# The last unit's exponentials and loads in another order, and the top-1 low-rank rows on four quarters of the partitions

## The chip, the cores and the metric

The kernel runs on one core of a Trainium2 chip. The core has five engines with queues of their own: TensorE (PE, and PEld for its weight loads), VectorE (DVE), ScalarE (ACT), GpSimd (POOL) and SyncE (SP), which here only issues DMAs. Each engine works through its own queue in order. The metric is device time in microseconds of one execution. The kernel before took 1837.35 us (median of three runs, 1833.86 to 1838.45).

## The reference

Two blocks in a row work on 1024 tokens of 512 features in fp32. The first is a linear-memory attention and a top-2 mixture of low-rank experts over a common dense matrix. The second, which matters here, is a state-space layer and a top-1 mixture:

```python
x = x + _L1_attn_ref(_layernorm(x), ...)   # state-space layer: 128 heads of 64, chunks of 128 tokens
x = x + _L1_ffn_ref(_layernorm(x), ...)    # 4 experts of rank 8, the best one per token
```

In the state-space layer the input is projected to a gate, to x, B and C (each with a causal convolution of 4 taps and a silu) and to time steps. With `A_cumsum`, the running sums of the time steps times A, it computes for each head

```python
Lmat = jnp.exp(segment_sum(Ac))                    # decays between positions of a chunk
M = Gm * jnp.transpose(Lmat, (0, 2, 3, 4, 1))      # times the products of C and B
Y_diag = jnp.einsum('bclsh,bcshp->bclhp', M, xch)
```

and adds what the chunk before hands on, scales by an RMS norm over all 8192 channels, multiplies by silu(gate) and projects back to 512 features. The mixture at the end is

```python
top1 = jnp.argmax(logits, axis=-1)
base_out = jnp.einsum('bth,oh->bto', x, W_up)
z = jnp.einsum('nh,erh->ner', x_flat, lora_A)      # 4 x 8 = 32 low-rank rows for each token
d = jnp.einsum('ner,ehr->neh', z, lora_B) * SCALE
delta = jnp.einsum('neh,ne->nh', d, one_hot)       # only the chosen expert's
```

## The kernel before

**Units.** The state-space layer runs as 72 units: eight groups, each with one "bc" unit (B and C) and eight "pair" units (two heads each). Units are staggered. While the loop of line 948 projects unit n (`stage_a`, seven products on sums of operands, L529), it multiplies unit n-2 (`stage_c`, L751 and L759) and finishes it (`stage_d`, L777 and L778), transposes unit n-1 (`stage_t`, L695, with L698 and L705 on VectorE) and computes its decays. The last unit is n = 71; units 69, 70 and 71 are all pair units.

**Decays.** For each pair unit a tile `cst` (128 x 2 x 12 x 128) is filled from HBM with the running sums by one broadcast DMA of 1536 KB (`load_sums`, L646, two buffers). `decays(n, part)` turns it into the decay matrix: parts 0 and 1 are eight Relus each with a bias (L728), part 2 is two exponentials on ScalarE (L734) and two products with the group's matrix on VectorE (L736). `stage_c` reads the result. In the steady state part 2 is traced at the end of unit n+1, behind the silus of `stage_a`.

**Output products.** The projection back is done over the units as well, as seven products per pair of output matrices (L836) in PSUM. `add_up` copies each to SBUF on ScalarE (L845, three buffers called `prod`) and POOL issues a DMA that accumulates it in HBM (L846, `prod_d`, 256 KB each). PSUM holds two of these products at a time (tag `mm1`). The last unit has the last seven products, of half m = 0: three are copied in its first half and four in its second. At the end `load_prods` reads the products back (L860, L861, four DMAs for each half m, on SP), and `put_together` adds them: m = 1 on POOL, m = 0 on VectorE (L868 to L874). The last four pairs do not go through these products; they are multiplied plainly after the units (`out_project`, L1040).

**The order of the work.** A planner lays out each engine's queue: it goes by the order in which the program traces the instructions and takes a later one first where an earlier one is not ready by its own costs. `issue_after(ins)` keeps what is traced inside it behind `ins` on the engine of `ins`; that is how the order is written out by hand. `last` holds the instructions that serve for this. `behind_keeps` holds silus of the convolution (L580) until `let_go` issues them behind the `keep` copies.

**After the units** come, in program order: the Relus of unit 71, its silu, the eight reads, stages C and D of unit 70, two pairs of `out_project` for four tiles of tokens, the transposes of unit 71, the third pair, `put_together(1)`, stages C and D of unit 71, `put_together(0)`, the rest of `out_project`, the sums for the RMS norm (L1068), and then per tile of 128 tokens the last pair, the read-back parts (L1082), the residual and a layer norm (`finish`).

**The mixture** is `lora_mixture` (L148). For each of eight tiles of tokens it computes logits and low-rank rows in one product (L160), copied to `lg` and `h`. `h` is 128 wide per tile, and for the last layer (32 rows) the rest is set to zero. `base` (L174) multiplies a tile with the dense matrix, four products of 128 x 512; three tiles are taken ahead. `route` finds the best expert, L187 zeroes the other experts' rows, eight transposes (L190) and one copy (L191) turn `h`, and one product per tile (L193) adds the low-rank part in the same PSUM bank as its base. L196 adds the residual and `store` writes the tile. `f1_up`, the 32 rows of `lora_B`, sits on the first 32 of 128 partitions, the rest zero (L1027). PSUM has eight banks: four under the tag `in`, two under `mm1` and one pair under `mm2`.

Of the kernel before, what the change touches and what calls it, by code (L numbers as in the profile page):

```python
# [28 lines left out]
F32 = mybir.dt.float32  # L29
AF = mybir.ActivationFunctionType  # L30
ALU = mybir.AluOpType
AX = mybir.AxisListType

P = 128
# [19 lines left out]
def model_kernel(ctx: ExitStack, tc: tile.TileContext, a: dict, out: bass.AP):  # L54
# [93 lines left out]
    def lora_mixture(name, E, R, w_base, w_cat, w_up, route, psum, pool, done, ready=None):  # L148

        ER = E * R  # L150
        lg = pool.tile([P, NT, E], F32, tag="lg", name=f"{name}_lg")
        h = pool.tile([P, NT, P], F32, tag="e", name=f"{name}_h")
        if ER < P:
            nc.gpsimd.memset(h, 0.0)
        for t in range(NT):
            if ready:
                ready(t)
            ps = psum.tile([P, 512], F32, tag="mm1", name=f"{name}_psl{t}")
            for k in range(KT):
                nc.tensor.matmul(  # L160
                    ps[:, : E + ER],
                    lhsT=xnT[:, k, toks(t)],
                    rhs=w_cat[:, k, :],
                    start=(k == 0),
                    stop=(k == KT - 1),
                )
            nc.vector.tensor_copy(lg[:, t, :], ps[:, :E])
            nc.vector.tensor_copy(h[:, t, :ER], ps[:, E : E + ER])
        hT = pool.tile([P, NTOK], F32, tag="sig", name=f"{name}_hT")
# [15 lines left out]
        cmb = route(lg)  # L185
        hv = h[:, :, :ER].rearrange("p t (e r) -> p t e r", r=R)
        nc.vector.tensor_tensor(hv, hv, cmb.unsqueeze(3).to_broadcast([P, NT, E, R]), ALU.mult)  # L187
# [4 lines left out]
        for t in range(NT):  # L192
            nc.tensor.matmul(held[t], lhsT=hT[:, toks(t)], rhs=w_up, start=False, stop=True)  # L193
            if t + ahead < NT:
                held[t + ahead] = base(t + ahead)
            nc.vector.tensor_tensor(x[t], held.pop(t), x[t], ALU.add)  # L196
            done(t)


# [155 lines left out]
    with ExitStack() as c1:  # L355
# [11 lines left out]

        last = {"pe": None, "one": None, "two": None, "adt": None, "bar": None, "keep": None, "cst": None, "silu": None}

# [270 lines left out]
        def load_sums(n):  # L640

            kind, j = units[n]
            if kind == "bc":
                return
            cst = b2.tile([P, 2, NT + NB, P], F32, tag="cst", name=f"cst{j}")
            nc.sync.dma_start(  # L646
                out=cst.rearrange("p h c l -> p h (c l)"),
                in_=cs_d[2 * j : 2 * j + 2, :].unsqueeze(0).to_broadcast([P, 2, (NT + NB) * P]),
            )
            held[n].update(cst=cst)  # L650
# [66 lines left out]
        def decays(n, part):  # L717
# [15 lines left out]
            for hh in range(2):  # L733
                nc.scalar.activation(mf[:, hh], mf[:, hh], AF.Exp, scale=-1.0)  # L734
            for hh in range(2):
# [212 lines left out]
        for n in range(len(units)):  # L948
# [22 lines left out]
            with issue_after(last["keep"]):  # L971
                add_up()
                if steady:
                    decays(n - 1, 1)
            turn(n, 1)
            next(a_steps)
            out_products(share - share // 2)
            add_up()
            if share and not todo:
# [14 lines left out]
        N = len(units)  # L994
        for part in range(2):
            decays(N - 1, part)
        let_go()
        load_prods(1)
        load_prods(0)
        with issue_after(last["pe"]):  # L1000
# [15 lines left out]
        class PsumF:  # L1016
            @staticmethod
            def tile(shape, dt, tag, name):
                if "ln_ps" in name or "psl" in name:
                    return two_banks[0][:, int("psl" in name)]  # L1020
                return Psum.tile(shape, dt, {"mm2": "mm2", "mm1": "in"}[tag], name)

# [3 lines left out]
        f1_up = b3.tile([P, DM], F32, tag="sg", name="f1_up")  # L1026
        nc.gpsimd.memset(f1_up, 0.0)  # L1027
        nc.sync.dma_start(out=f1_up[:32, :], in_=a["f1_up"])
        x_v = x_d.rearrange("(t p) d -> p t d", p=P)
# [129 lines left out]
```

## Time and profile before

| What | Value |
|---|---|
| Median of three runs | 1837.35 us (1833.86 to 1838.45) |
| Profiled execution | 1835.83 us, of which the span is 1834.0 us |
| Mean granted TensorE clock | 0.993 |
| TensorE busy | 1787.6 us, 97% of the span |
| VectorE, ScalarE, POOL busy | 1295.6, 1195.4, 713.2 us |
| TensorE's longest single wait | 9.1 us, `ps_y` L751 for `cst` L736, until 1736.6 |
| From the last logits product (about 1800.7) to the end | 33 us |

Times inside the span are in microseconds from its start. A row of the order of time gives start, duration, engine, line, instruction, tile written and tiles read, and in brackets the engine's idle time before it with what ended it. Where instructions of a kind follow each other, they are merged and counted (x8). An fp32 matmul shows as two records, and records of matmuls overlap, so that their durations add up to more than the time they take together. A row of windows gives a stretch, its length, for each engine the busy time and the number of instructions, the clock granted to TensorE as a share of full speed, the busy share of the DMA engines and the rate that they moved.

### The profile page before, as it was taken

The numbers are of one execution on the slowest core, as the hardware profiler recorded it, in microseconds if no ns is written. First come the engines' busy times: TensorE is split into PE (matmuls) and PEld (weight loads), VectorE is DVE, ScalarE is ACT, GpSimd is POOL, SyncE is SP. The second block draws the span as 40 slices with busy tenths as digits, with TensorE's granted clock in tenths as the row PEclk, the third lists the DMA queues.
The fourth block names the chain that finished last, engine by engine and source line by source line (L and its number), as shares of the span: only waits on it lengthen the run. The fifth ranks groups of instructions, "written<-read, shape, count | busy, mean of one in ns | idle before, by whom it ended". The sixth has DMA issues, their size and how long they took to land.

```text
span 1834.0 us, 21364 instructions
## 1 busy us (share of the span) xinstructions
PE 1787.6 (97%) x7670; PEld 940.2 (51%) x7670; DVE 1295.6 (71%) x1470; ACT 1195.4 (65%) x2145; POOL 713.2 (39%) x691
## 2 busy tenths in 40 slices
PE   7999988999999999999999999999999999999799
PEld 4545544555555555555555555545555555555464
DVE  4524798876777777767877687867786877587462
ACT  4311259776878588847875787678766876687730
POOL 5410242344444444443345434534453444443310
PEclk9999999999999999999999999999999999999899
DMA  8100133454466555555565556554655565556811
GB/s 318 65 1 10 49 127 125 154 156 111 121 163 151 134 138 144 144 144 143 147 152 144 109 152 156 145 133 116 149 147 141 147 146 144 110 147 169 213 48 46
DMA packets 81338, 241.05 MB, mean 131 GB/s; under 512 B 9584, under 2 KB 10608, under 8 KB 71888
## 3 DMA queue, kind: packets, MB, share of 16 engines
q1 hardware_dynamic: 48768, 171.49, 27.0%
q0 software_dynamic: 31888, 67.14, 22.2%
q8 instruction: 61, 1.00, 0.2%
q10 hardware_dynamic: 576, 1.05, 0.2%
q14 instruction: 45, 0.37, 0.1%
HBM read 177.78 MB, written 61.87 MB: 131 GB/s over the span
## 4 chain that ended last, share of the span: by engine, by line
PE 88%; DVE 5%; ACT 3%; DMA 2%; issue 1%; POOL 1%; SPq 0%; DVEq 0%; POOLq 0%; ACTq 0%
PE pa L529 25%; PE ps_p L836 19%; PE pd L529 12%; PE pb L529 6%; PE ps_y L751 5%; PE f_pso L174 3%; PE ps_q L97 3%; PE ps_o L309 3%; PE ps_xt L695 3%; PE ps_y L759 2%; DVE xT L572 1%; ACT cst L728 1%; DMA cst<-cs_d 1%; PE f_pso L193 1%; DMA prod_d<-prod 1%
## 5 line engine op out<-in xcount | busy, mean ns | idle before, releaser
L846 POOL DMA_DIRECT2D prod_d<-prod x217 | 190.3, 915 | 575.7 <-ACT prod L845 554.4
L728 ACT ACTIVATE cst<-cst,cs 128x128 f32<-128x128 f32 x1024 | 313.0, 398 | 4.5 <-DMA cst<-cs_d 4.5
L572 DVE SCALAR_TENSOR_TENSOR xT<-raw,convw,xT 128x1020 f32<-128x1020 f32 (+2 forms) x216 | 278.1, 1289 | 4.1
L736 DVE TENSOR_TENSOR cst<-cst,gt 128x1536 f32<-128x1536 f32 x128 | 221.2, 1756 | 19.3 <-ACT cst L734 19.1
L514 POOL TENSOR_TENSOR wsum<-win 128x256 f32<-128x256 f32 x72 | 112.3, 1560 | 265.8 <-DMA win<-in_win 223.6
L769 ACT ACTIVATE xdt<-xT 128x1024 f32<-128x1024 f32 x64 | 67.7, 1058 | 197.7 <-DVE xT L767 197.7
L734 ACT ACTIVATE cst<-cst 128x1536 f32<-128x1536 f32 x128 | 189.5, 1484 | 1.0
L751 PE MATMUL ps_y<-cst,xdt 128*64 128x128 f32 x2048 | 161.6, 278 | 11.2 <-DVE cst L736 9.1
L836 PE MATMUL ps_p<-xT,wout 128*128 128x512 f32 x360 | 165.0, 593 | 0.1
L552 DVE TENSOR_TENSOR raw<-pb,keep 128x512 f32<-128x512 f32 x72 | 49.6, 689 | 161.2 <-PE pb L529 158.1
L556 DVE TENSOR_TENSOR raw<-pd,keep 128x512 f32<-128x512 f32 x72 | 49.7, 690 | 157.0 <-PE pd L529 129.4
L751 PEld LDWEIGHTS ps_y<-cst,xdt 128*64 128x64 f32 x2048 | 120.2, 138 | 60.8 <-issue 50.7
L540 ACT COPY keep<-pa 128x512 f32<-128x512 f32 x144 | 84.7, 588 | 101.2 <-PE pa L529 101.2
L529 PE MATMUL pa<-xnT,wsum 128*128 128x512 f32 x288 | 144.7, 626 | 4.5 <-ACT keep L540 4.5
L845 ACT COPY prod<-ps_p 128x512 f32<-128x512 f32 x217 | 122.5, 580 | 38.7 <-PE ps_p L836 17.3
L529 PE MATMUL pa<-tok,win 128*128 128x512 f32 x288 | 135.7, 593 | 1.9 <-DVE sg L559 1.9
L529 PE MATMUL pd<-tok,wsum 128*128 128x512 f32 x288 | 137.0, 593 | 0.0
L529 PE MATMUL pa<-xnT,win 128*128 128x512 f32 x288 | 135.8, 592 | 0.6 <-DVE raw L552 0.6
L529 PE MATMUL pa<-tok,wsum 128*128 128x512 f32 x288 | 135.5, 593 | 0.7 <-POOL wsum L517 0.5
L529 PE MATMUL pd<-xnT,wsum 128*128 128x512 f32 x288 | 135.5, 592 | 0.0
L529 PE MATMUL pb<-xnT,win 128*128 128x512 f32 x288 | 135.3, 592 | 0.0
L836 PE MATMUL ps_p<-ysum,osum 128*128 128x512 f32 x240 | 112.8, 592 | 0.0
(217 smaller groups left out, 3144.8 us busy)
## 6 DMA issues: line engine op xcount, KB each, us to landing
cst<-cs_d SPq DMA_DIRECT2D x64, 1536.0 KB, 7.4
prod_d<-prod POOLq DMA_DIRECT2D x217, 256.0 KB, 5.0
win<-in_win SPq DMA_DIRECT2D x144, 256.0 KB, 3.3
wout<-in_wout SPq DMA_DIRECT2D x64, 256.0 KB, 4.2
wo_s<-in_wo POOLq DMA_DIRECT2D x8, 1024.0 KB, 5.8
out<-prod_d SPq DMA_DIRECT2D x6, 512.0 KB, 5.2
wq<-in_wq SPq DMA_DIRECT2D x8, 256.0 KB, 4.7
x_d<-x SPq DMA_DIRECT2D x8, 256.0 KB, 2.0
```

The source lines that it names most:

```text
L514: op(v[:, 0], w[:, 1, 0:2], w[:, 1, 2:4], ALU.add)
L529: last["pe"] = nc.tensor.matmul(ps, lhsT=wt[:, k, :], rhs=tk[:, k, :], start=start and k == 0, stop=k == 1, skip_group_check=not start,)
L540: last["keep"] = nc.scalar.copy(c, ps)
L572: nc.vector.scalar_tensor_tensor(d[:, :, k:], src[:, :, : SEQ - k], convw[:, i, TAPS - 1 - k : TAPS - k], d[:, :, k:], ALU.mult, ALU.add,)
L728: nc.scalar.activation(m[:, part, c, :], m[:, part, c, :], AF.Relu, bias=cs[:, c, h : h + 1], scale=1.0)
L734: nc.scalar.activation(mf[:, hh], mf[:, hh], AF.Exp, scale=-1.0)
L736: last["cst"] = nc.vector.tensor_tensor(mf[:, hh], mf[:, hh], gr.rearrange("p c l -> p (c l)"), ALU.mult)
L751: last["pe"] = nc.tensor.matmul(flat(py)[e, toks(c)], lhsT=xdt[:, c, e], rhs=m[:, hh, c, :], start=True, stop=c % 2 == 0,)
L769: nc.scalar.activation(sq, y, AF.Square)
L836: last["pe"] = nc.tensor.matmul(ps, lhsT=w, rhs=y, start=i == over[0], stop=i == over[-1])
L845: nc.scalar.copy(st, ps)
L846: nc.gpsimd.dma_start(out=prod_d[m][p // 2][p % 2], in_=st, accum_op=ALU.add if over[0] else ALU.bypass)
```

## The change

In the last unit four things move. The exponentials and products of unit 70's decays (`decays(n - 1, 2)`) are traced before stage C of unit 69. The copies of the last four products are kept behind those exponentials on ScalarE. After the loop unit 71's silu comes ahead of its Relus, each behind the other, where the Relus came first. The eight reads of the products are kept behind the last load of sums on the SP queue.

In the last mixture `h` is 32 wide per tile without zeros, and `mix_rows` takes over after the logits. It transposes four tiles at once, so that their low-rank rows come to lie on four quarters of the partitions; `f1_up` is loaded four times, once per quarter. Tiles 0 and 1 have their bases ahead of the routing, tiles 2 and 3 behind the transposes; then come the eight low-rank products, each on 32 partitions and in a PSUM bank of its own, and then the bases of tiles 6, 4, 5 and 7, which add onto them.

```diff
-        h = pool.tile([P, NT, P], F32, tag="e", name=f"{name}_h")
-        if ER < P:
-            nc.gpsimd.memset(h, 0.0)
+        h = pool.tile([P, NT, ER], F32, tag="e", name=f"{name}_h")
...
+        if ER == 32:
+            mix_rows(name, E, R, h, lg, w_base, w_up, route, psum, pool, done)
+            return
...
+    def mix_rows(name, E, R, h, lg, w_base, w_up, route, psum, pool, done):
+        G = 4
+        hT = pool.tile([P, NT // G, P], F32, tag="sig", name=f"{name}_hT")
+        mm1 = lambda t: psum.tile([P, 512], F32, tag="mm1", name=f"{name}_pso{t}")
+        held = {}
+
+        def base(t):
+            more = t in held
+            ps = held[t] = held[t] if more else mm1(t)
+            for k in range(KT):
+                nc.tensor.matmul(
+                    ps,
+                    lhsT=xnT[:, k, toks(t)],
+                    rhs=w_base[k // 2][:, k % 2, :],
+                    start=k == 0 and not more,
+                    stop=k == KT - 1 and more,
+                )
+
+        def up(t, first):
+            r = slice(t % G * 32, t % G * 32 + 32)
+            nc.tensor.matmul(held[t], lhsT=hT[r, t // G, :], rhs=w_up[r, :], start=first, stop=not first)
+
+        def add(t):
+            nc.vector.tensor_tensor(x[t], held.pop(t), x[t], ALU.add)
+            done(t)
+
+        base(0)
+        base(1)
+        cmb = route(lg)
+        hv = h.rearrange("p t (e r) -> p t e r", r=R)
+        nc.vector.tensor_tensor(hv, hv, cmb.unsqueeze(3).to_broadcast([P, NT, E, R]), ALU.mult)
+        pt = psum.tile([P, 2, 512], F32, tag="mm2", name=f"{name}_psT")
+        for q in range(NT // G):
+            nc.tensor.transpose(
+                pt[:, 0, toks(q)], h[:, q * G : (q + 1) * G, :].rearrange("p t r -> p (t r)"), ident
+            )
+        nc.scalar.copy(hT, pt[:, 0, : NT // G * P].rearrange("p (q t) -> p q t", t=P))
+        base(2)
+        base(3)
+        for t in range(G):
+            up(t, False)
+        rest = psum.tile([P, 2, 512], F32, tag="mm2", name=f"{name}_rest")
+        for t in range(G, NT):
+            held[t] = rest[:, t % 2, :] if t >= NT - 2 else psum.tile([P, 512], F32, tag="two", name=f"{name}_pso{t}")
+            up(t, True)
+        for t in range(G):
+            add(t)
+        for t in (NT - 2, *range(G, NT - 2), NT - 1):
+            base(t)
+            add(t)
...
-            nc.sync.dma_start(
+            last["sums"] = nc.sync.dma_start(
                 out=cst.rearrange("p h c l -> p h (c l)"),
...
-                nc.scalar.activation(mf[:, hh], mf[:, hh], AF.Exp, scale=-1.0)
+                last["exp"] = nc.scalar.activation(mf[:, hh], mf[:, hh], AF.Exp, scale=-1.0)
...
+            if n == len(units) - 1:
+                decays(n - 1, 2)
             turn(n, 1)
             next(a_steps)
             out_products(share - share // 2)
-            add_up()
+            with issue_after(last["exp"] if n == len(units) - 1 else None):
+                add_up()
...
-        for part in range(2):
-            decays(N - 1, part)
-        let_go()
-        load_prods(1)
-        load_prods(0)
+        with issue_after(last["silu"]):
+            for step in behind_keeps:
+                last["silu"] = step()
+        behind_keeps.clear()
+        with issue_after(last["silu"]):
+            for part in range(2):
+                decays(N - 1, part)
+        with issue_after(last["sums"]):
+            load_prods(1)
+            load_prods(0)
...
-                return Psum.tile(shape, dt, {"mm2": "mm2", "mm1": "in"}[tag], name)
+                return Psum.tile(shape, dt, {"mm2": "mm2", "mm1": "in", "two": "mm1"}[tag], name)
...
-        nc.gpsimd.memset(f1_up, 0.0)
-        nc.sync.dma_start(out=f1_up[:32, :], in_=a["f1_up"])
+        for q in range(4):
+            nc.sync.dma_start(out=f1_up[q * 32 : (q + 1) * 32, :], in_=a["f1_up"])
```

More of the change, by code (lines that the diff above doesn't have):

```diff
@@ L167, in lora_mixture @@
             nc.vector.tensor_copy(lg[:, t, :], ps[:, :E])
-            nc.vector.tensor_copy(h[:, t, :ER], ps[:, E : E + ER])
+            nc.vector.tensor_copy(h[:, t, :], ps[:, E : E + ER])
+        if ER == 32:
+            mix_rows(name, E, R, h, lg, w_base, w_up, route, psum, pool, done)
+            return
         hT = pool.tile([P, NTOK], F32, tag="sig", name=f"{name}_hT")
@@ L185, in lora_mixture @@
         cmb = route(lg)
-        hv = h[:, :, :ER].rearrange("p t (e r) -> p t e r", r=R)
+        hv = h.rearrange("p t (e r) -> p t e r", r=R)
         nc.vector.tensor_tensor(hv, hv, cmb.unsqueeze(3).to_broadcast([P, NT, E, R]), ALU.mult)
@@ L197, in lora_mixture @@
             done(t)
+    def mix_rows(name, E, R, h, lg, w_base, w_up, route, psum, pool, done):
[23 more added lines that the diff above has]
+        cmb = route(lg)
+        hv = h.rearrange("p t (e r) -> p t e r", r=R)
+        nc.vector.tensor_tensor(hv, hv, cmb.unsqueeze(3).to_broadcast([P, NT, E, R]), ALU.mult)
[18 more added lines that the diff above has]
+            add(t)
     with ExitStack() as c0:
@@ L364, in tile @@
                 return {"mm2": psum2, "mm1": psum1, "in": psumi}[tag].tile(shape, dt, tag=tag, name=name)
-        last = {"pe": None, "one": None, "two": None, "adt": None, "bar": None, "keep": None, "cst": None, "silu": None}
+        last = {"pe": None, "one": None, "two": None, "adt": None, "bar": None, "keep": None, "cst": None, "silu": None, "exp": None, "sums": None}
         def issue_after(ins):
```

## The prediction

> **What bounds the kernel now.** I read the page's shares of time first (TensorE is busy for 97% of the span, so only a stretch where it stands still, or TensorE work that goes, can move the end), then the waits of the last units, then those stretches engine by engine. One wait stands out: in the last unit (n = 71) TensorE waits 9.1 us for the second half of unit 70's decay matrix `cst`. Windows (us busy and instructions of PE, PEld, DVE, ACT, POOL, then granted clock, DMA share, GB/s):
>
> ```profile
> PE ps_y L751 <- DVE cst L736: 9.1, 1, 9.1
> ...
> 1725.00:1736.60 11.60, 0.42 (x3) 0.19 (x2) 3.68 (x3) 7.76 (x14) 1.72 (x2) 0.66 1.05 289
> 1736.60:1739.00 2.40, 2.39 (x22) 2.40 (x24) 0.00 (x0) 2.40 (x9) 0.26 (x1) 0.50 1.02 395
> 1762.00:1800.70 38.70, 38.37 (x219) 27.19 (x220) 16.51 (x56) 12.87 (x25) 0.00 (x0) 1.00 0.00 1
> ```
>
> TensorE does 0.42 of 11.6 us, and the clock it then gets is 0.50. Later it is full. Why it waits is in the order of time of ScalarE, VectorE and the SP queue:
>
> ```profile
> 1719.35 1.06 ACT L769 ACTIVATE xdt<-xT 128x1024 f32<-128x1024 f32 x1 [4.63 <-DVE xT L767]
> ...
> 1723.73 1.48 ACT L734 ACTIVATE cst<-cst 128x1536 f32<-128x1536 f32 x1
> ...
> 1729.48 0.59 ACT L845 COPY prod<-ps_p 128x512 f32<-128x512 f32 x1 [3.79 <-DMA prod_d<-prod]
> 1730.09 1.28 ACT L634 ACT_TABLE_LOAD   x1
> ...
> 1731.98 1.28 ACT L734 ACT_TABLE_LOAD   x1
> 1733.28 1.48 ACT L734 ACTIVATE cst<-cst 128x1536 f32<-128x1536 f32 x1
> ```
>
> ```profile
> 1725.25 1.76 DVE L736 TENSOR_TENSOR cst<-cst,gt 128x1536 f32<-128x1536 f32 x1
> 1734.79 1.76 DVE L736 TENSOR_TENSOR cst<-cst,gt 128x1536 f32<-128x1536 f32 x1 [7.79 <-ACT cst L734]
> ```
>
> ```profile
> SPq L860 <- DMA prod_d<-prod: 8.4, 1, 8.4
> SPq L646 <- PE ps_p L836: 0.3, 1, 0.3
> ```
>
> The two exponentials (L734) stand 9.5 us apart: between them lie the last product copy, which waits for a product write to free its buffer, and two table loads. The reader should also see 4.63 us of idle ScalarE before 1719.35, and that unit 71's load of sums (L646, issued at 1721.77) stood on the SP queue behind a product read that waited 8.4 us, though its buffer was free when unit 69's matmuls ended at about 1716.6. The tail behind the last logits matmul:
>
> ```profile
> L174 PE MATMUL f_pso<-f_base,xnT 128*128 128x512 f32 x50 | 22.7, 594 | 0.0
> L193 PE MATMUL f_pso<-f_up,f_hT 128*128 128x512 f32 x16 | 7.8, 592 | 0.0
> L196 DVE TENSOR_TENSOR xr<-f_pso,xr 128x512 f32<-128x512 f32 x8 | 5.5, 692 | 22.5 <-PE f_pso L193 22.5
> L190 PE MATMUL f_psT<-ident,f_h 128*128 128x128 f32 x8 | 1.0, 272 | 0.0
> ```
>
> TensorE has no idle there, so what it no longer does comes off the end. An fp32 matmul leaves two records, one started every 0.43 us (66 of L174 and L193 from 1800.68 to 1829.97, less 0.87 for L190).
>
> **Exponentials first.** Two L734 and their two L736 move ahead of stage C of unit 69 in the program. Unit 70's last Relu ends at 1714.73; a table load (1.28) and two exponentials (1.48 each) then end at 1719.0, inside ScalarE's idle time. On VectorE the two L736 pass L767 of unit 69, L559, the last tap L572, L777, L778 and unit 70's L698 and L705. These are late by up to 2 x 1.7 = 3.4 us; behind L559 waits the last projection of unit 71, behind L767 the transposes L695, both with TensorE idle after them. VectorE worked without a gap from 1713.92 to 1727.0 with one L736 in it; with the other it ends at 1728.7, and stage C of unit 70 starts there instead of at 1736.61: **-7.9**. If the idle cover on ScalarE is gone (square L769 first), the exponentials come 1 to 2 us later and VectorE's sum stays the same.
>
> The clock: TensorE fell idle at 1725.0 and the granted clock fell at 1728.7, 3.7 us later; it was full again at 1742.4. Now idle runs from about 1725.4 (L559 later) to 1728.2, under 3 us, so I take no drop. Stage C of unit 70 took 5.31 us at half clock, of unit 69 2.84: **-2.5**; its bounds are -2.5 and 0.
>
> So TensorE could reach unit 71's stage C (1753.63 before) after 1728.7 + 2.8 for stage C, + 11.7 for the output matmuls L1040 and the transposes L695 (1741.92 to 1753.63) = 1743.2. What is late next is unit 71's own `cst`. The copies now wait for the exponentials (no cost: the first ran at 1720.32, they end at 1719.0). The last copy still waits for the write of three copies before; I leave it at 1729.5 to 1730, as writes took 4.4 to 9.1 us in this stretch and DMA is as full. Then L634 0.5, silu L580 1.0 (no table load: the silus are now adjacent, and of the five table loads from 1722.44 to 1741.82 two go), 16 Relus 4.7, table load and two exponentials 4.2: 1740.9. VectorE does L736, L698, L705, L736 from 1739.4: + 1.7 + 1.2 + 0.6 + 1.7 = 1744.6. I take **1744.7 against 1753.63: -8.9**. Bounds: -10.4 (TensorE alone, the copy no hindrance) and -5 (copy at 1733.5). From there to L1068 (8.7 us, PE with 0.5 wait) and through 38.7 us of finishing nothing changes.
>
> **Sums ahead of reads.** L646 can go at about 1716.7, 5 us earlier; Relus then no longer wait for it (9.6 us to landing gives 1726.3). The eight reads go behind it: the first from 1704.41 to about 1717.1. Behind that read waits POOL's addition L868 (1713.20 before), and behind L868, if it is ahead on POOL, the writes L846. The first three writes gain (they stood behind L868 from 1710 to 1714.4); the last four may lose. I put zero in the sum, and price it as a rival. The additions L868 to L874 on POOL have until 1757, and the second set, on VectorE, follows L736 as before.
>
> **Low-rank rows.** Transposes: 2 for 8, 6 x 0.109 = **-0.65**. The copy L191 gets 256 columns for 1024 (1.01 us before, under the 0.59 of a 512-column copy), beside base matmuls. The eight `up` products keep 16 records of 512 columns. On separate partition quarters they may run side by side; no row here shows that for rows. The bounds are 16 x 0.43 = 6.9 us (no overlap) and a quarter, 1.7. The nearest row is stage C: two 64-column halves, 48 records of 128 columns in 2.77 us, 0.058 each, against 0.11 for L1082's full ones, an overlap by all of its factor. I take 1.8 us (16 weight loads at 0.11): **-5.1**. [...] I allow **+0.3** for entering and leaving the quarters (0.17 us idle after stage C of unit 69). Only two tiles' bases stand ahead of the routing now, not three: two records were left at 1800.68, and the routing ended at 1802.68. If no later base is put there, TensorE stands 1.2 us; half of that, **+0.6**. The last store: the last three came 0.86 us apart and the end lies 3.3 us behind the last addition; stores alone landed in 2.0, and now each has 3.4 us of base matmuls before it: **-1.0**.
>
> **At nothing:** two POOL memsets (0.53, 0.95, POOL idle after 1747.9). Three more loads of `f1_up` on SP, 3 x 0.35 = 1.05 us, ahead of the second residual load (1756.50, first needed at about 1774): uncovered, they would cost that 1.05.
>
> **Sum:** -8.9 - 0.65 - 5.1 + 0.3 + 0.6 - 1.0 = -14.75. The profiled execution took 1835.83 (span 1834.0 and 1.8 around it), 1.5 below the median of 1837.35 and within the three runs: **1821.1**, say 1821.
>
> **Rivals.**
> A. The last copy slips. If L868 stands ahead of the last four writes on POOL, the first of them goes at about 1727.5 instead of 1721.2 (read landing 1726, addition 1.26). The last copy then comes at about 1735 and unit 71 at 1749.5: -4.1 in front, in all -10: 1826. For it: before, L868 stood ahead of three writes whose first copy had ended at 1710.5, and they went from 1714.4. Against: it is ready later now.
> B. The quarters run one after another: ups 6.9, in all -9.65: 1826. For: no row of row quarters. Against: the column halves overlap.
> C. Slower. All seven additions of the first set stand ahead of those writes: third read at 1730, 8.9 us of additions to 1739, write to 1748, copy there, unit 71's stage C at 1762.5; TensorE idle for over 3.7 us, so half clock again, +2.5: 1765, front +11.4, in all +5.6: 1841. It ends on this side from a last copy later than about 1742 (without the clock loss 1745): there the front's loss passes the tail's 5.85. Against: the writes of the first four products are ready before the later reads.
> D. The exponentials do not move up in the queue (the order is the planner's): tail alone, -5.85: 1830.
>
> **Chances.** Forecast 0.58, A 0.15, B 0.13, C 0.08, D 0.06. 0.3% (5.5 us from the median, 1831.8) is about what a measurement can tell from no change. Faster: forecast, A, B and most of D, 0.84; same 0.08 (some of D and C); slower 0.08. Range: at the low end front -10.4, ups at a quarter, no stall (about 1818.5) and 2 us of run spread, 1816; at the high end A and B are in, and D at its edge: 1830.
>
> **What would show it.** Both L734 of unit 70 before 1720 and adjacent; the 9.1 us wait gone, and granted clock 1.00 in stage C of unit 70, starting near 1729; L646 near 1717; stage C of unit 71 near 1745; 16 records of the `up` products within about 2 us. Wrong it would be if the wait on `cst` came back at unit 71 with a product copy before it, or if those records start 0.43 us apart.

## The result and the profile after

The changed kernel took 1824.06 us (median of six runs, 1823.64 to 1826.26), against 1836.17 us of the kernel before beside it (six runs, 1833.86 to 1838.45): a ratio of 0.9936, 95% interval 0.9923 to 0.9949, or 12 us less. The prediction said 1821, range 1816 to 1830. The profiled execution took 1823.95 us (span 1822.2) and is compared with the profiled 1835.83 (span 1834.0) of before: -11.9, where the sum had -14.75. Profiles, and what is read from them below, are of one execution of each kernel. Line numbers of the changed kernel are higher: the exponential L734 is L788, its product L736 L790, stage C L751 and L759 are L805 and L813, L767, L769, L777, L778 are L821, L823, L831, L832, the copy L845 is L899, POOL's writes L900, the additions L922 to L928, the sums' load L646 is L700, the reads L914 and L915, `out_project` L1102, the RMS sums L1130. In the mixture the logits L160 are L158, the base is L212, the transposes L235, the low-rank products L222.

The waits of TensorE in the last units, after (engine, line and what it waited for; us in total, times, longest):

```profile
PE ps_y L805 <- issue: 3.7, 2, 2.5
PE ps_out L1102 <- DVE xT L831: 1.3, 1, 1.3
PE ps_y L805 <- DVE cst L790: 1.2, 1, 1.2
```

The 9.1 us on `cst` are gone. In their place stand four smaller waits, 6.2 us together, where before 2.1 and 0.5 stood beside the long one. The order of time of ScalarE, VectorE, the SP queue and POOL, after, shows what moved:

```profile
1711.84 1.48 ACT L788 ACTIVATE cst<-cst 128x1536 f32<-128x1536 f32 x1
...
1716.66 1.49 ACT L788 ACTIVATE cst<-cst 128x1536 f32<-128x1536 f32 x1
...
1727.63 0.59 ACT L899 COPY prod<-ps_p 128x512 f32<-128x512 f32 x1 [4.33 <-DMA prod_d<-prod]
...
1729.55 4.77 ACT L782 ACTIVATE cst<-cst,cs 128x128 f32<-128x128 f32 x16
1734.22 1.04 ACT L823 ACTIVATE xdt<-xT 128x1024 f32<-128x1024 f32 x1
...
1736.58 2.86 ACT L788 ACTIVATE cst<-cst 128x1536 f32<-128x1536 f32 x2
```

```profile
1725.19 2.58 DVE L626 SCALAR_TENSOR_TENSOR xT<-raw,convw,xT 128x1016 f32<-128x1016 f32 x2
...
1735.30 2.14 DVE L831 SCALAR_TENSOR_TENSOR xT<-xT,normw,sg 128x1024 f32<-128x1024 f32 x1 [5.76 <-ACT xdt L823]
1737.37 2.30 DVE L832 TENSOR_TENSOR ssq<-ssq,xdt 128x1024 f32<-128x1024 f32 x1
...
1741.32 3.98 DVE L790 TENSOR_TENSOR cst<-cst,gt 128x1536 f32<-128x1536 f32 x2
```

```profile
1716.21 0.33 SPq L700 DMA_DIRECT2D cst<-cs_d  x1
```

```profile
1736.33 2.25 POOL L927 TENSOR_TENSOR out<-out 128x512 f32<-128x512 f32 x1
1738.54 2.26 POOL L926 TENSOR_TENSOR out<-out,out 128x512 f32<-128x512 f32 x1
```

Unit 70's two exponentials run at 1711.84 and 1716.66, with a copy, a `keep` and the last Relus between them, where they ran at 1723.73 and 1733.28. The load of sums leaves at 1716.21. What the reader should see besides is the square L823 of unit 70: it stands behind all sixteen Relus of unit 71, and VectorE does nothing for 5.76 us until it ends; then L831, L832 and the L790 pair each take longer than the 1.28, 1.22 and 3.5 that such rows take elsewhere, and POOL's additions beside them take 2.25 where the rows next to them take 1.27.

TensorE's order of time after, at the two stages C and in the tail, and its windows (us busy and instructions of PE, PEld, DVE, ACT, POOL, then granted clock, DMA share, GB/s):

```profile
1725.38 0.66 PE L805 MATMUL ps_y<-cst,xdt 128*64 128x128 f32 x8 [1.18 <-issue]
...
1737.50 3.70 PE L1102 MATMUL ps_out<-wout,xT 128*128 128x512 f32 x8 [1.34 <-DVE xT L831]
1743.73 0.40 PE L805 MATMUL ps_y<-cst,xdt 128*64 128x128 f32 x2 [2.53 <-issue]
1745.35 0.90 PE L805 MATMUL ps_y<-cst,xdt 128*64 128x128 f32 x5 [1.22 <-DVE cst L790]
...
1756.13 1.84 PE L1130 MATMUL two_banks<-ones,ssq 128*128 128x1 f32 x16
...
1793.43 0.98 PE L158 MATMUL two_banks<-f_cat,xnT 128*128 128x36 f32 x8
1794.24 2.82 PE L212 MATMUL f_pso<-f_base,xnT 128*128 128x512 f32 x6
1796.90 0.38 PE L235 MATMUL f_psT<-ident,f_h 128*128 128x128 f32 x2
1797.12 5.32 PE L212 MATMUL f_pso<-f_base,xnT 128*128 128x512 f32 x12
1802.37 1.56 PE L222 MATMUL f_pso<-f_up,f_hT 32*128 32x512 f32 x10
...
1804.29 3.70 PE L212 MATMUL f_rest<-f_base,xnT 128*128 128x512 f32 x8
...
1814.70 3.60 PE L212 MATMUL f_rest<-f_base,xnT 128*128 128x512 f32 x8
```

```profile
1725.40:1728.20 2.80, 2.80 (x49) 2.63 (x49) 2.34 (x2) 0.57 (x2) 0.00 (x0) 1.00 1.11 248
...
1741.05:1744.40 3.35, 0.55 (x3) 0.19 (x2) 3.35 (x3) 0.00 (x0) 0.97 (x1) 0.99 0.94 264
...
1745.35:1750.66 5.31, 5.31 (x46) 4.98 (x46) 3.14 (x5) 0.00 (x0) 0.00 (x0) 0.50 0.31 91
```

Stage C of unit 70 starts at 1725.38 and runs at full clock. Stage C of unit 71 starts in earnest at 1745.35, 8.3 us earlier than before, but at half clock: 5.31 us where 2.8 are enough. The half clock did not go, it moved from one unit to the next.

One quantity carries the rest: the time from the start of unit 69's stage C to the RMS sums. Before it was 1713.75 to 1762.33, 48.58 us; after it is 1713.33 to 1756.13, 42.80. So the front gave -5.78. The tail, from the end of the last logits product to TensorE's end, went from 29.29 (1800.68 to 1829.97) to 23.89 (1794.41 to 1818.30): -5.40. With -0.42 that already stood ahead of unit 69's stage C, -0.07 between the sums and the tail and -0.1 behind TensorE's end this is -11.8, the difference of the spans.

### The profile page after: what moved, and what is told of

It is laid out like the page before. It is cut to its first block, busy times and chain, and to the rows that moved or that the text cites. A ratio compares the mean times of both kernels' runs of the same rounds, so it can differ in the third digit from the quotient of the medians.

```text
span 1822.2 us, 21347 instructions
## 1 busy us (share of the span) xinstructions
PE 1781.4 (98%) x7664; PEld 937.8 (51%) x7664; DVE 1294.7 (71%) x1470; ACT 1192.0 (65%) x2143; POOL 712.3 (39%) x689
## 4 chain that ended last, share of the span: by engine, by line
PE 87%; DVE 4%; ACT 3%; issue 2%; DMA 2%; POOL 1%; SPq 0%; DVEq 0%; POOLq 0%; ACTq 0%
PE pa L583 25%; PE ps_p L890 18%; PE pd L583 12%; PE pb L583 6%; PE ps_y L805 5%; PE ps_q L97 3%; PE ps_o L363 3%; PE ps_xt L749 3%; PE ps_y L813 2%; PE f_pso L175 2%; DVE xT L626 1%; PE f_pso L212 1%; ACT cst L782 1%; PE ps_out L1102 1%; DMA cst<-cs_d 1%
## 5 line engine op out<-in xcount | busy, mean ns | idle before, releaser
L900 POOL DMA_DIRECT2D prod_d<-prod x217 | 190.2, 909 | 584.5 <-ACT prod L899 552.1
L626 DVE SCALAR_TENSOR_TENSOR xT<-raw,convw,xT 128x1020 f32<-128x1020 f32 (+2 forms) x216 | 278.1, 1289 | 4.1
L790 DVE TENSOR_TENSOR cst<-cst,gt 128x1536 f32<-128x1536 f32 x128 | 221.2, 1757 | 13.1 <-ACT cst L788 13.0
L823 ACT ACTIVATE xdt<-xT 128x1024 f32<-128x1024 f32 x64 | 67.7, 1058 | 194.5 <-DVE xT L821 194.5
L788 ACT ACTIVATE cst<-cst 128x1536 f32<-128x1536 f32 x128 | 189.5, 1484 | 1.0
L805 PE MATMUL ps_y<-cst,xdt 128*64 128x128 f32 x2048 | 162.5, 279 | 4.9 <-issue 3.7
L805 PEld LDWEIGHTS ps_y<-cst,xdt 128*64 128x64 f32 x2048 | 120.9, 139 | 54.5 <-issue 52.3
L899 ACT COPY prod<-ps_p 128x512 f32<-128x512 f32 x217 | 122.4, 580 | 38.7 <-PE ps_p L890 17.9
L854 POOL TENSOR_TENSOR osum<-wout,wout 128x256 f32<-128x256 f32 x30 | 103.1, 3437 | 26.0 <-DMA wout<-in_wout 25.6
```

Source lines behind the costliest of these rows:

```text
L626: nc.vector.scalar_tensor_tensor(d[:, :, k:], src[:, :, : SEQ - k], convw[:, i, TAPS - 1 - k : TAPS - k], d[:, :, k:], ALU.mult, ALU.add,)
L788: last["exp"] = nc.scalar.activation(mf[:, hh], mf[:, hh], AF.Exp, scale=-1.0)
L790: last["cst"] = nc.vector.tensor_tensor(mf[:, hh], mf[:, hh], gr.rearrange("p c l -> p (c l)"), ALU.mult)
L805: last["pe"] = nc.tensor.matmul(flat(py)[e, toks(c)], lhsT=xdt[:, c, e], rhs=m[:, hh, c, :], start=True, stop=c % 2 == 0,)
L854: op(v[:, 0], e[:, 256:], o[:, 256:], ALU.add)
L899: nc.scalar.copy(st, ps)
```

## The experiments

The theory: front and tail act apart and add up; the front's gain comes from the exponentials and a little from the load; it fell short because the square is late and POOL's additions slow VectorE, so that TensorE idles ahead of unit 71's stage C and pays for it in clock; the tail's gain is the overlap of four quarters. Rivals: the gain lies in only one half; the edge on the reads or the clock makes it; the low-rank products gain by something else than quarters; and the lost microseconds move on to another wait whatever is mended. "Front" below is the time from unit 69's stage C to the RMS sums in each kernel's own trace, one execution each. It differs between executions of the same instructions: `after`, `one_quarter` and `all_rows` are alike up to the sums and have 42.80, 43.16 and 44.20, and `before` and `tail_only`, alike there in the order of the work, 48.58 and 47.81. A difference of 1.4 us or less is therefore not shown by fronts.

| Kernel | Median us (runs) | Ratio to before, 95% interval | Front us |
|---|---|---|---|
| before | 1836.17 (6) | | 48.58 |
| after | 1824.06 (6) | 0.9936, 0.9923 to 0.9949 | 42.80 |
| front_only | 1830.34 (9) | 0.9971, 0.9961 to 0.9981 | 42.72 |
| tail_only | 1830.51 (6) | 0.9972, 0.9961 to 0.9984 | 47.81 |
| exp_back | 1828.40 (4) | 0.9959, 0.9945 to 0.9972 | 47.43 |
| no_sums_edge | 1825.33 (4) | 0.9940, 0.9927 to 0.9954 | 45.02 |
| one_quarter | 1836.36 (1) | | 43.16 |
| all_rows | 1829.34 (1) | | 44.20 |
| square_first | 1822.90 (5) | 0.9935, 0.9921 to 0.9948 | 39.97 |
| no_pool_adds | 1815.85 (1) | | 36.48 |
| square_fill_ssq | 1823.79 (5) | 0.9931, 0.9917 to 0.9944 | 38.55 |
| square_split | 1821.81 (4) | 0.9922, 0.9908 to 0.9935 | 39.39 |
| fill_split | 1821.59 (5) | 0.9920, 0.9907 to 0.9934 | 37.46 |
| all_vector | 1817.30 (4) | 0.9895, 0.9879 to 0.9912 | 36.74 |

**The two halves.** `front_only` is the kernel before with the changes of order alone, `tail_only` the changed kernel with those undone (the diff is that of `tail_only`; `front_only` has the complement).

```diff
-            if n == len(units) - 1:
-                decays(n - 1, 2)
             turn(n, 1)
...
-            with issue_after(last["exp"] if n == len(units) - 1 else None):
-                add_up()
+            add_up()
...
-        with issue_after(last["silu"]):
-            for step in behind_keeps:
-                last["silu"] = step()
-        behind_keeps.clear()
-        with issue_after(last["silu"]):
-            for part in range(2):
-                decays(N - 1, part)
-        with issue_after(last["sums"]):
-            load_prods(1)
-            load_prods(0)
+        for part in range(2):
+            decays(N - 1, part)
+        let_go()
+        load_prods(1)
+        load_prods(0)
```

> The change in the last unit alone, with the mixture of the kernel before. If the two halves of the change act apart: the front's share as the two profiles give it, L1068 about 5.8 us earlier (6.2 between the profiles, of which 0.4 lies ahead of anything that changed), so 1835.8 - 5.8 = 1830 us. If they need each other (the mixture's bases as work that fills gaps, the shorter h on VectorE), it differs by more than 1.5 us from that.

> The mixture on quarters alone, with the order of the last unit of the kernel before. Acting apart: 5.2 us less behind the last logits product, 1830.5 us, the 9.1 us wait on the decay matrix still there. If the halves need each other, more than 1.5 us away from that.

Measured: -0.29% and -0.28%, together -0.57% beside the whole's -0.64% with intervals of about 0.1% each. The halves add up; neither hides the other. The front of `front_only`, 42.72, is that of the whole.

**The exponentials alone put back.** `exp_back` undoes the first two edits of that diff and keeps the silu ahead of the Relus, the load and the tail.

```diff
-            if n == len(units) - 1:
-                decays(n - 1, 2)
             turn(n, 1)
...
-            with issue_after(last["exp"] if n == len(units) - 1 else None):
-                add_up()
+            add_up()
```

> The changed kernel without the moved exponentials (and without the copies held behind them); the reads still go behind the last load of sums, and unit 71's silu ahead of its Relus. Theory 1 (the exponentials' move is the gain in the last unit): the two exponentials of unit 70 stand apart again with a product copy between them, TensorE waits about 9 us for the second half of the decay matrix, and nearly all of the 5.8 us is lost: about 1829.5 us. Theory 2 (the earlier load of sums is what gains): 1825 us or less.

The old wait is back in TensorE's waits of `exp_back`, and its front is 47.43:

```profile
PE ps_y L805 <- DVE cst L790: 8.9, 1, 8.9
```

So of the 5.78 the exponentials' place, with the copies held behind them, is worth 4.6, and 4.3 us in the time (1828.40 against 1824.06).

**The reads not held behind the load of sums.**

```diff
-        with issue_after(last["sums"]):
-            load_prods(1)
-            load_prods(0)
+        load_prods(1)
+        load_prods(0)
```

> The changed kernel without the reads held behind the last load of sums: on SP the load stands behind four reads again, and on POOL the first addition behind the first read stands ahead of the first product write. Theory 1 (the load was early enough to matter): it goes out at about 1721.5 instead of 1716.2 and lands at about 1730.5, so unit 71's Relus start 1 to 2 us after the last copy would let them, and the kernel takes 1 to 2 us more, 1825 to 1826 us. Theory 2 (the last product copy, at 1727.6, holds the Relus anyway, and the reads moved behind the load cost as much): 1824 us, within 0.5.

The load left at 1720.03 instead of 1716.21 and landed after 11.1 us; unit 71's Relus waited for it, in ScalarE's order of time:

```profile
1731.19 4.78 ACT L782 ACTIVATE cst<-cst,cs 128x128 f32<-128x128 f32 x16 [2.76 <-DMA cst<-cs_d]
```

The front is 2.2 us longer, the time 1.3, within the intervals: the edge is the smaller part, and that it gains at all is seen in the Relus' wait and not in the time. POOL's first addition here ran at 1711.80, ahead of three writes; with the edge it ran at 1729.08, behind all of them, so the order that rivals A and C needed did not arise in the changed kernel.

**The low-rank products on one quarter.** `one_quarter` takes the rows of the first quarter for every tile, so the low-rank part is another tile's for six of eight; the number and the size of the products are the same, and all lie on one quarter.

```diff
-            r = slice(t % G * 32, t % G * 32 + 32)
+            r = slice(0, 32)
```

> The changed kernel, but all eight low-rank products read the first quarter of the partitions (so every tile gets the rows of tile 0 or 4 and the output is another). Theory 1 (products on different quarters run side by side): on one quarter the 16 records start 0.43 us apart, 6.9 us instead of 1.9, 5 us more in all: 1829 us. Theory 2 (a product over 32 rows is short by itself): still about 2 us, 1824 us.

TensorE's order of time and windows, `one_quarter`:

```profile
1802.89 7.65 PE L222 MATMUL f_pso<-f_up,f_hT 32*128 32x512 f32 x12
1810.34 3.62 PE L222 MATMUL f_rest<-f_up,f_hT 32*128 32x512 f32 x4
1813.88 6.51 PE L212 MATMUL f_rest<-f_base,xnT 128*128 128x512 f32 x8
```

```profile
1802.90:1805.00 2.10, 2.10 (x6) 1.03 (x6) 0.78 (x2) 0.00 (x0) 0.00 (x0) 1.00 0.00 0
1805.00:1810.00 5.00, 5.00 (x8) 2.04 (x7) 1.99 (x3) 0.00 (x0) 0.00 (x0) 0.59 0.56 210
```

The products do not overlap: at full clock the first 2.10 us hold six records, where `after` has all 16 in 1.92. That confirms where the gain is from: in `after` the four of a set start within 0.02 us of each other. But here they took 11.0 us and not 16 x 0.43 = 6.9, which neither theory had: the granted clock fell to 0.50 while TensorE worked without a gap, and the bases behind them paid too (6.51 for 3.7). Was it the 32 rows, or the run of products? `all_rows` takes all 128 partitions, which adds the rows of three other tiles to each product:

```diff
-            r = slice(t % G * 32, t % G * 32 + 32)
+            r = slice(0, 128)
```

> The up products of the last mixture take all 128 partitions of the copied rows and of the weights instead of one tile's 32; this changes what is computed in them (each tile gets the rows of four), so only their time is read. Theory 1 (the clock fell in one_quarter because products of 32 rows, one at a time, keep too little of the array at work): 16 records 0.43 us apart, 6.9 us, granted clock 1.00 through it, base products of the pair that follows at 3.7 us, time about 1829. Theory 2 (the clock falls there for another reason, such as eight products with a new accumulator each in a row): 16 records in about 11 us, granted clock 0.5 to 0.6 between 1805 and 1812, about 1836.

TensorE's order of time, `all_rows`:

```profile
1802.93 5.31 PE L222 MATMUL f_pso<-f_up,f_hT 128*128 128x512 f32 x12
1808.08 1.88 PE L222 MATMUL f_rest<-f_up,f_hT 128*128 128x512 f32 x4
1809.80 3.60 PE L212 MATMUL f_rest<-f_base,xnT 128*128 128x512 f32 x8
```

1802.93 to 1809.80 is 6.87 us for 16 records, the clock 1.00 throughout, the time 1829.34 with 1829 expected. Only the number of rows differs between the two, one execution each: the 32-row products, one at a time, ended at 0.50, the 128-row ones at 1.00. On four quarters at once (1802.37 to 1804.29, 1.92 us) it was 1.00 too.

**The square ahead of the Relus.** Unit 70's stage C and its square are traced ahead of unit 71's Relus.

```diff
-            nc.scalar.activation(sq, y, AF.Square)
+            last["sq"] = nc.scalar.activation(sq, y, AF.Square)
...
-        with issue_after(last["silu"]):
+        with issue_after(last["pe"]):
+            stage_c(N - 2)
+        with issue_after(last["sq"]):
             for part in range(2):
                 decays(N - 1, part)
...
-        with issue_after(last["pe"]):
-            stage_c(N - 2)
-            stage_d(N - 2)
+        stage_d(N - 2)
```

> The changed kernel, with the square of unit 70 ahead of unit 71's sixteen Relus on ScalarE, and these behind it. Theory 1 (the square standing behind the Relus holds up normw on unit 70, and with it VectorE's whole queue, so unit 71's stage C starts late and at half clock): normw of unit 70 at about 1731 instead of 1735.3, the second product on unit 71's decay matrix done at about 1741.6 instead of 1745.3, stage C of unit 71 in 2.8 us at full clock instead of 5.3, the RMS sums at about 1750 instead of 1756.1: 1818 us. Theory 2 (VectorE is slow there because POOL adds beside it, or unit 71's exponentials come too late): stage C of unit 71 starts within 1 us of where it does now, 1823 to 1824 us.

L831 moved up from 1735.30 to 1730.72, but the front gained 2.8 and not 6. The median, 1822.90 for 1818 expected, is 1.2 us below that of the changed kernel and within the intervals, so by itself the square's place is shown in the trace and not in the time. VectorE's and POOL's order of time, `square_first`:

```profile
1738.18 4.61 DVE L790 TENSOR_TENSOR cst<-cst,gt 128x1536 f32<-128x1536 f32 x2 [0.32 <-ACT cst L788]
1742.71 1.76 DVE L922 TENSOR_TENSOR out<-out 128x512 f32<-128x512 f32 x1
1744.39 1.75 DVE L923 TENSOR_TENSOR out<-out,out 128x512 f32<-128x512 f32 x1
1746.18 0.69 DVE L924 TENSOR_TENSOR out<-out,out 128x512 f32<-128x512 f32 x1
```

```profile
1737.17 1.27 POOL L925 TENSOR_TENSOR out<-out,out 128x512 f32<-128x512 f32 x1
1738.40 2.78 POOL L927 TENSOR_TENSOR out<-out 128x512 f32<-128x512 f32 x1
1741.14 2.79 POOL L926 TENSOR_TENSOR out<-out,out 128x512 f32<-128x512 f32 x1
1743.88 1.72 POOL L928 TENSOR_TENSOR out<-out,out 128x512 f32<-128x512 f32 x1
```

Where VectorE's products and POOL's additions lie side by side, both are longer (4.61 us for the pair, 2.78 and 2.79 for an addition of POOL), and the same additions are 0.69 and 1.27 apart from each other. The clock fell here too, at 1744.0 in the middle of stage C. To test the contention, `no_pool_adds` is `square_first` without POOL's seven additions (the sum of the half m = 1 is left out, its loads are not):

```diff
             g = prods[m]
+            if m:
+                return [[g[1], g[2]], [g[3], g[6]]]
```

> The kernel with the square ahead of the Relus, but without the seven additions on POOL (left out; the output lacks them). Theory 1 (VectorE's two decay products of unit 71 are slowed by the additions that POOL does beside them): they take 1.76 us each instead of 2.3, the second ends at about 1741.7 instead of 1742.8, and the first two additions on VectorE take 0.69 each instead of 1.76. Theory 2 (something else slows VectorE there, as the transfers into the same memory): 2.3 and 1.76 us as before.

VectorE's order of time, `no_pool_adds`:

```profile
1736.33 3.43 DVE L790 TENSOR_TENSOR cst<-cst,gt 128x1536 f32<-128x1536 f32 x2 [0.15 <-ACT cst L788]
```

The pair is back at 3.43, stage C of unit 71 ran at full clock, and the front is 36.48. What POOL costs VectorE there, with the clock that it costs TensorE, is 3.5 us of the front, in one execution.

**Filling TensorE's idle time.** `square_fill_ssq` is `square_first` with three output products of one tile ahead of unit 71's stage C, and the sum of squares ahead of the norm weight in the last unit.

```diff
+        with issue_after(last["pe"]):
+            for t in range(4, 5):
+                for j in range(NPAIR - 4, NPAIR - 1):
+                    out_project(t, j, "in")
         with issue_after(last["pe"]):
             stage_c(N - 1)
             stage_d(N - 1)
...
+                if n == len(units) - 1:
+                    nc.vector.tensor_tensor(ssq, ssq, sq, ALU.add)
                 nc.vector.scalar_tensor_tensor(y, y, normw[:, j : j + 1], sg, ALU.mult, ALU.mult)
-                nc.vector.tensor_tensor(ssq, ssq, sq, ALU.add)
+                if n < len(units) - 1:
+                    nc.vector.tensor_tensor(ssq, ssq, sq, ALU.add)
```

> The kernel with the square ahead of the Relus, and three output products of the fifth tile of tokens moved ahead of unit 71's stage C, and in that stage the sum of squares ahead of normw. Theory 1 (TensorE's idle time ahead of stage C is what halves its clock): TensorE stands still for less than 1 us there, stage C of unit 71 takes 2.8 us at full clock and ends near 1746, and since VectorE then sets the RMS sums (its order: decay products, additions, stage C, sum of squares), they come at about 1751.8 instead of 1753.1: 1.3 us less than with the square alone. Theory 2 (the clock falls there for another reason): stage C takes 5 us again and no time is gained.

TensorE's order of time and windows, `square_fill_ssq`:

```profile
1743.97 0.54 PE L805 MATMUL ps_y<-cst,xdt 128*64 128x128 f32 x5 [0.71 <-DVE cst L790]
1746.74 2.84 PE L1105 MATMUL ps_out<-wout,xT 128*128 128x512 f32 x6
1752.61 3.51 PE L1137 MATMUL two_banks<-ones,ssq 128*128 128x1 f32 x16 [3.03 <-DVE ssq L832]
```

```profile
1743.90:1746.70 2.80, 2.73 (x46) 2.59 (x46) 2.77 (x4) 0.00 (x0) 1.16 (x1) 1.00 1.03 309
1752.60:1758.70 6.10, 6.09 (x23) 5.07 (x24) 1.26 (x2) 0.27 (x1) 0.00 (x0) 0.50 0.01 3
```

Stage C took 2.8 us at full clock, but the work that had been moved ahead of it was missing ahead of the sums: 3.03 us idle there, and the half clock with it. The time, 1823.79, is that of the changed kernel, though the front is 4.3 us shorter: from the sums to the end of the last logits product it is 41.64 us here and 38.28 in `after`, and the front does not hold that part. The loss had only moved.

**VectorE's own additions put later.** `square_split` keeps the sum of squares ahead, drops the filling, and lets five of VectorE's seven additions wait for the D term of unit 71; `fill_split` has the filling too.

```diff
-            nc.vector.scalar_tensor_tensor(y, y, dd[:, j : j + 1], flat(py), ALU.mult, ALU.add)
+            last["yd"] = nc.vector.scalar_tensor_tensor(y, y, dd[:, j : j + 1], flat(py), ALU.mult, ALU.add)
...
             op(g[5], g[0], g[5], ALU.add)
+            with issue_after(None if m else last["yd"]):
+                return put_rest(g, op)
```

> As square_fill_ssq (square of unit 70 ahead of the Relus, three output products of one tile ahead of stage C of unit 71, sum of squares ahead of the norm weight in the last unit), and of the seven POOL additions only the first two stand right behind the last decay product; the other five wait for the addition of the D term in unit 71. Theory 1 (the front came out at -5.8 because the square stood behind the Relus and POOL's additions slowed VectorE's last operations, and what TensorE then idles costs clock too; with both causes gone the front gives the -8.9 and more): the L790 pair of unit 70 back near 3.5 to 4 us, sums of the RMS norm 36 to 37 us behind the start of stage C of unit 69 (after: 42.8), granted clock not at 0.50 between 1740 and 1757, time 1818 to 1820. Theory 2 (the loss only moves: a wait of 3 us or more of TensorE and half clock come back somewhere ahead of the sums whichever operation is moved): sums at 38.5 or more, 1822 to 1824.

> The same without the three output products ahead of stage C of unit 71. Theory 1 (contention with POOL made VectorE late; without it stage C of unit 71 is early enough that TensorE idles under 3 us and needs no filling): stage C of unit 71 near 1740 to 1741, sums at 36.5 to 37.5 us behind stage C of unit 69, 1818 to 1820. Theory 2 (TensorE still idles long enough for the clock to fall in that stage): granted clock 0.50 in it, sums at 39 to 40, about 1822.

Neither came to the 1818 to 1820 expected: `fill_split` took 1821.59, `square_split` 1821.81. POOL's additions still lay beside the L790 pair, which took 5.63 and 4.90 us, and the clock fell in both, in `square_split` at 1747.1 inside stage C, in `fill_split` at 1751.8 among the sums. The edit is not the one expected: the first of the two texts speaks of POOL's additions, and the edit puts off VectorE's. So Theory 1 is not tested by it.

**POOL's additions on VectorE.** `all_vector` is `square_first` with the sum of squares ahead and all fourteen additions on VectorE: four behind the last L790, ten behind the D term of unit 71.

```diff
-            op = (nc.gpsimd if m else nc.vector).tensor_tensor
+            op = lambda o, x, y, kind=ALU.add: nc.vector.tensor_tensor(g[o], g[x], g[y], kind)
...
-        parts = {1: put_together(1)}
+        parts = {}
...
         with issue_after(last["cst"]):
-            parts[0] = put_together(0)
+            put_together(1, 0)
+        with issue_after(last["yd"]):
+            put_together(0, 0)
+            for m in (1, 0):
+                parts[m] = put_together(m, 1)
```

> As square_first, with POOL's seven product additions done by VectorE instead (four behind the last decay product, ten behind the D term of unit 71) and the sum of squares ahead of the norm weight in the last unit. Theory 1 (what kept the front from its size was POOL's additions beside VectorE's decay products, and TensorE's idle time that came of it): the L790 pair of unit 71 in about 3.5 us, stage C of unit 71 near 1740 at full clock, sums of the RMS norm 36 to 37 us behind the start of stage C of unit 69 (after: 42.8), nothing at 0.50 between 1740 and 1760, time 1816 to 1819. Theory 2 (the loss moves on: VectorE, now with seven additions more, 4.8 us, makes the finishing stage wait, or the clock falls elsewhere): sums at 36 to 37 but TensorE idle 2 us or more behind them, or clock 0.50 there, 1820 to 1823.

VectorE's order of time and TensorE's windows, `all_vector` (L924 is every addition):

```profile
1738.41 3.43 DVE L790 TENSOR_TENSOR cst<-cst,gt 128x1536 f32<-128x1536 f32 x2 [0.56 <-ACT cst L788]
...
1742.36 2.14 DVE L924 TENSOR_TENSOR out<-out,out 128x512 f32<-128x512 f32 x3
```

```profile
1738.00:1743.00 5.00, 2.94 (x26) 1.66 (x26) 4.59 (x4) 1.75 (x2) 0.00 (x0) 1.00 1.02 346
1743.00:1748.00 5.00, 5.00 (x38) 3.11 (x35) 4.66 (x7) 1.90 (x2) 0.00 (x0) 1.00 1.00 325
1748.00:1753.00 5.00, 5.00 (x27) 3.37 (x26) 5.00 (x8) 0.70 (x2) 0.00 (x0) 1.00 0.37 140
```

Median 1817.30 us (1816.75 to 1817.58), ratio 0.9895, interval 0.9879 to 0.9912: faster than before and, by intervals that do not meet, than the changed kernel (0.9923 to 0.9949). Nothing at half clock there, front 36.74, the pair at 3.43. VectorE does seven additions more and the end still comes earlier, since TensorE has work without a gap from 1742 on. Against `square_first` three things differ; `square_split` has the other two in part (the sum of squares ahead, five of VectorE's additions late) and took 1821.81, so most of the 5.6 us go with POOL's additions.

## Why the prediction was right, and where it was off

The direction, the two halves and their sources came as forecast. Term by term:

- **Exponentials and stage C of unit 70 (-7.9, -2.5): the mechanism shown, the time better.** 1725.38 instead of 1728.7: the sum let the stage wait for all of VectorE's work, but the two last taps (L626, 2.58 us) stood behind `xdt` and `xdr`, which the stage needs. Full clock, 2.8 us; that it held is in part luck, since TensorE idled 1.18 us and not the 2.8 that I had priced at nothing (in the same trace the clock fell at 1744.30, with 2.53 us of idle time ahead of unit 71's stage C).
- **Front, -8.9: the mis-sized term, -5.78 measured.** The second product on unit 71's `cst` let TensorE go on at 1745.35, forecast 1744.7. The step that failed lies behind it: "From there to L1068 ... nothing changes". It was 8.70 us before and is 10.78 now. I had worked out that TensorE would be ready at 1743.2 and `cst` at 1744.7, and priced the wait but not what it does to the clock: -2.5 was booked for unit 70 and the same 2.5 had to be paid in unit 71; 0.5 of it came back as the wait of L1068 went. -8.28 (1753.63 to 1745.35) + 2.08 is -6.2, of which 0.42 stood ahead of unit 69.
- **What made `cst` late was not what I had named, and that its time came out within 0.7 us is luck.** The list of ScalarE's work ended with exponentials at 1740.9, from a last copy at 1729.5. The copy came at 1727.63, two table loads went as counted, and the exponentials ended at 1739.4; the square L823, which I had left out of that list, stands among them. On VectorE, L831 waited 5.76 us for it, and L831, L832 and L790 were 2.4 us longer beside POOL's additions (2.14 + 2.30 + 3.98 against 1.28 + 1.22 + 3.5). The earlier copy and these two delays about cancelled out. The profile before already had such rows: beside POOL's L874 (2.79 us from 1745.12, for 1.27) L736 took 2.15 and L777 2.28, for 1.76 and 1.28. The prediction gave those additions "until 1757" and so no price: it asked when they must end and not what they run beside. `no_pool_adds` and `all_vector` put that price, with the square and the clock, at 6 us of the front.
- **Sums ahead of reads, zero:** the load left at 1716.21 (1716.7 forecast); by `no_sums_edge` it is worth 1.3 us in time (within the intervals) and 2.2 in front, since without it the Relus wait 2.76 us for the load.
- **Rows, -0.65 and -5.1, +0.3, +0.6.** 16 records in 1.92 us, where 1.8 and 0.3 for entering and leaving the quarters stood: the overlap is 6.9 / 1.92 = 3.6-fold. Both were estimates: the 0.11 for a weight load is the spacing of L1082's products, where the records of L193's loads have 0.19 in the trace of before, and no run shows the 0.3 by itself. What the runs showed is the 1.92 in all. The stall behind the routing did not come: of the six base records from 1794.24 two belong to the first two tiles (14 of their 16 stood ahead) and four to a third, and these filled the time until the transposes. Together -5.40 against -4.85.
- **Last store, -1.0: wrong, -0.1 measured.** The end lies 3.2 us behind the last addition, before 3.3. The store lands in 2.0 in both, so there was no queueing among stores to save; after, the rest (1821.06 to 1822.2) holds only semaphores and drains.
- **Rivals.** A and C: every write stood ahead of POOL's first addition (1729.08). B: refuted by the 1.92 us, and `one_quarter` shows what it would have been, worse than its 6.9. D: the exponentials moved, and `exp_back` is the kernel in which they don't.

The 1.8 us that I took amount to a 3.8-fold overlap; the trace shows 3.6. The sets of four start 0.43 to 0.53 us apart, about one product's 0.43, so within a set the overlap is all of its factor and some 0.2 us stand at the two ends.

## What to carry to other kernels

When a long wait of TensorE goes, look for the next wait and price it twice, for its length and for the clock: here the 2.5 us of full clock gained in unit 70's stage C were paid in unit 71's, after 2.53 us of idle time. An engine with time to spare is not free to be used: ask what its work runs beside, as here VectorE's L790 pair took 3.98 to 5.63 us beside POOL's additions and 3.43 without them, and with the seven on VectorE (and the sum of squares ahead) the kernel took 1817.30 us, for 1822.90 in `square_first`. A stage is late by the last thing in its chain, so list every instruction of each queue in between, the short ones too: here one square of 1 us behind sixteen Relus held VectorE for 5.8.

## What the runs showed of the hardware

**Half clock came in stretches of 3.41, 6.8 and 13.7 us.** Times of a fall and of the return, worked out from windows of 0.2 to 1 us that hold both clocks: before 1728.74 and 1742.40 (13.66 apart), after 1744.30 and 1751.14 (6.84), `square_first` 1744.03 and 1747.44 (3.41), `square_split` 1747.12 and 1750.54 (3.42), `fill_split` 1751.80 and 1758.62 (6.82), `one_quarter` 1805.92 and 1819.58 (13.66): one, two or four times 3.41. An early fall of the trace of before, at 271.25 (a window from 271 to 272 has 0.62), is 1457.49 ahead of 1728.74, or 427 times 3.4133.

**Ahead of a fall TensorE had mostly done little, and not always in one idle piece.** In the traces of before and after, the 3.41 us ahead of each of the seven falls inside the span have 0.24 to 1.30 us of TensorE's records. After, it was 0.71 ahead of the fall in unit 71 (1740.89 to 1744.30), in two pieces with 2.53 of idle time between; in `square_first` 1.16 of 3.40, and the fall then came in the middle of a stage that already ran. Two falls came with more: in `one_quarter` TensorE never stopped, but worked on a quarter of the rows; in `fill_split` it did 2.19 of 3.40, of which 1.42 were the sums for the RMS norm, products of one column. And `all_vector` stayed at 1.00 with 0.44 us of work in the 2.50 from 1739.40. The step of the prediction, idle under 3 us and so no drop, was an estimate from one fall, 3.7 us behind the start of an idle time; the fall after 2.53 us shows that it does not carry over.

The mean clocks of the six runs of `after` are 0.994 to 0.997: one kernel lost more clock in one run than in another.

**VectorE and POOL side by side took almost the sum of their times.** In `square_first`, from 1738.18 to 1746.14, VectorE did the L790 pair and two additions, 3.43 + 2 x 0.68 us where they run alone, and POOL three additions of 1.27: 8.6 us of work, in 7.96 us. Without any slowing it would have been 4.8. One row does not show it: after, L752, which reads PSUM (`ps_xt`) and one tile of SBUF, ran beside POOL's L926 (1739.59) and took its usual 1.21.
